# A graph network's first batch in another order: key chunks, adjacency rows, and who evicts

## The chip, the cores and the metric

The program runs on one core of a Trainium2 chip. The core has five engines that each work through their own list of instructions in order: TensorE (PE: matmuls and transposes; its weight loads are listed as PEld), VectorE (DVE), ScalarE (ACT), GpSimd (POOL) and SyncE (SP), which here only issues transfers. SBUF is the working memory, PSUM holds what TensorE writes. The metric is the device time of one execution in microseconds (us).

## The reference

Two layers over 16 graphs of 1024 nodes with 256 features. The adjacency matrix is symmetric, with ones on the diagonal. Every layer starts with `h = relu(layernorm(x))`.

```python
# layer 0
qkv = layer_norm(h, gamma1, beta1)            # 8 heads of 32
scores = qkv @ qkv.T / sqrt(32)               # by head
attn = softmax(where(adj > 0, scores, -inf))
h = h + attn @ qkv
y = layer_norm(h, gamma2, beta2)
x = x + h + gelu(y @ W1 + b1) @ W2 + b2
# layer 1
h = relu(layernorm(x))
t = h @ W
logits = (t @ a_1).T + t @ a_2 + (t @ a_12) @ t.T
att = softmax(where(adj > 0, leaky_relu(logits, 0.2), -9e15))
x = x + elu(h @ W_1 + (att @ h) @ W_2)
```

Queries, keys and values of layer 0 are one matrix, so its scores are symmetric.

## The kernel before

`fast_path` does the work; a second function is there for inputs that the first can't serve, and does not run. All 16 batches are written out one after another in one instruction stream, and the order that the program writes is kept on every engine.

**Units.** The attention of layer 0 goes in units. A unit is one half of the queries (512), one group of four heads and one tile of 128 keys: `scores` makes four blocks of 128 x 512 scores in two PSUM tiles, adds the mask, and takes exponentials; `weigh` multiplies the exponentials of the unit before with the values. Batch 0 has 32 units (2 query halves x 2 groups x 8 key tiles). In each of them TensorE adds the mask to the first two heads by a matmul with an identity, and VectorE adds it to the other two (line 1070); ScalarE takes the four exponentials (line 1077). Each of the two PSUM score tiles has one buffer. From batch 1 on the second half of the scores is taken from the symmetry ("mirrored"), VectorE adds all masks, and the units share TensorE with the matmuls of the MLP and of layer 1 of the batch before, which fill its time. Batch 0 has no batch before it.

**Preparing a batch** (`prologue`). The 1024 rows are four chunks of 256. For a chunk: `load`, `measure` "a" (statistics of x on VectorE, small steps on GpSimd), `rectify` (ScalarE: the normalized, clipped h), `measure` "b" (statistics of h), `value` (VectorE normalizes; GpSimd scales by gamma1 and adds beta1 into `va`), `turn` (TensorE transposes, ScalarE copies into `kT`). For chunks 0 and 1 of batch 0 `turn_normed` transposes before the scaling, ScalarE scales on the way out of PSUM, and GpSimd makes `va` afterwards (lines 838 to 853). Units 0 to 15 of batch 0 use queries of chunks 0 and 1; key tiles 4 to 7 (chunks 2 and 3) come from unit 4 on.

**Masks.** `fetch_mask` loads a tile of 128 adjacency rows as two halves of 256 KB; there are two such buffers. `convert_mask` (line 594, VectorE) makes 8-bit masks in `mq`, which has one buffer for a half of the queries (four tiles). A transposing transfer on SyncE turns each tile into `mk`. `turn_masks` does this for four tiles in six pieces: fetch 0; conversion 0 and fetch 1; transpose 0, conversion 1 and fetch 2; and so on. The first half of batch 0 has its own way, in `prologue`: four tiles of whole rows, 512 KB each, are loaded (`fetch`, line 884) and converted (`convert`, line 887). `compare_masks` then has GpSimd subtract mask and transposed mask (line 964); `collect` reduces the difference, by a square on ScalarE for the first half of the queries and by a maximum on VectorE for the second.

**Setup.** `setup` loads the weights and forms products of W, a_1, a_2 and a_12, with small evictions from PSUM on ScalarE (lines 678, 694).

**The order.** Each kind of work is a stream that yields places, and the piece with the lowest place is written next. Batch b's attention has places b to b + 1; in batch 0 one unit is 1/32 = 0.03125. `stream_c` places the preparation (that of batch 1 in 32 pieces from 0.34 to 0.85), `stream_m` the masks, `stream_s` the setup (0.25, 0.30, 0.35). `spread` lays n pieces between two places. Beside that, `defer` holds short follow-ups (a collection after a comparison: 3.0) until a planner's clock has gone on by so much; a unit of batch 0 counts 2.45. SyncE's transfers wait in SyncE's list for the buffers they need.

Of the kernel before, what the change touches and what calls it, by code (L numbers as in the profile page):

```python
# [495 lines left out]
def fast_path(  # L496
# [168 lines left out]
    def setup():  # L665
# [8 lines left out]
        for oc in range(DC):  # L674
            pt = ps_tile([P, DC, P], f"p_wT_{oc}")
            for ic in range(DC):
                nc.tensor.transpose(pt[:, ic, :], wl[:, ic, oc * P : (oc + 1) * P], ident)
            nc.scalar.copy(wT[:, oc, :], pt.rearrange("p c q -> p (c q)"))
        clock[0] += 0.5
        yield  # L680

        def product(dst, lhs, rhs, n, name):

            for oc in range(DC):
                pp = ps_tile([P, n], f"p_{name}_{oc}")
                for kc in range(DC):
                    matmul(
                        pp,
                        lhs[:, kc, oc * P : (oc + 1) * P],
                        rhs[:, kc, :n],  # L690
                        start=(kc == 0),
                        stop=(kc == DC - 1),
                    )
                nc.scalar.copy(dst[:, oc, :], pp)

        product(wb, wa, wT, D, "wb")
        clock[0] += 1.7
# [95 lines left out]
    def prologue(b, st):  # L793
# [30 lines left out]
        def value(i):  # L824
            mv, rs = stats["b", i]
            for j in range(TPC):
                t = i * TPC + j
                nrm = tmpp.tile([P, D], F32, tag="w1", bufs=6, name=f"nrm_{b}_{t}")
                normalize(nrm, h[t // TPH][:, t % TPH, :], mv, rs, j)
                if b == 0 and i < 2:  # L830
                    normed[t] = nrm
                    continue
                nc.gpsimd.tensor_mul(nrm, nrm, g1)  # L833
                nc.gpsimd.tensor_add(va[:, t, :], nrm, be1)
# [3 lines left out]
        def turn_normed(i):  # L838
# [7 lines left out]
            for g in range(NG):  # L846
                nc.scalar.activation(
                    kT[:, g, i * CW : (i + 1) * CW], pt[:, g, :], AF.Identity, bias=be1c[:, g : g + 1], scale=g1c[:, g : g + 1]
                )
            for j in range(TPC):  # L850
                t = i * TPC + j
                nc.gpsimd.tensor_mul(va[:, t, :], normed[t], g1)
                nc.gpsimd.tensor_add(va[:, t, :], va[:, t, :], be1)

        def turn(i):
            clock[0] += 0.5
            pt = ps_tile([P, NG, CW], f"ptk_{b}_{i}")
            for g in range(NG):
                for j in range(TPC):
                    nc.tensor.transpose(  # L860
                        pt[:, g, j * P : (j + 1) * P], va[:, i * TPC + j, g * P : (g + 1) * P], ident
                    )
            nc.scalar.copy(kT[:, :, i * CW : (i + 1) * CW], pt)

        steps = [
            load,
# [8 lines left out]
        if b == 0:  # L875
# [15 lines left out]

            load(0)
            load(1)
            for t in range(TPH):
                fetch(t)
                if t == 0:
                    for tile, src in first_rows:
                        nc.sync.dma_start(tile, src)
            load(2)
            load(3)  # L900
            measure(0, "a")
            measure(1, "a")
            rectify(0)
            rectify(1)
            measure(0, "b")
            measure(1, "b")
            value(0)
            turn_normed(0)
            convert(0)
            value(1)  # L910
            turn_normed(1)
            convert(1)
            convert(2)
            convert(3)
            yield
            for f in (lambda i: measure(i, "a"), rectify):
                for i in (2, 3):
                    f(i)
            yield
            measure(2, "b")  # L920
            value(2)
            yield
            measure(3, "b")
            value(3)
            yield
            for i in (2, 3):
                turns.append((1, lambda i=i: turn(i)))
                yield
            return
        for k in range(NCH + len(steps) - 1):  # L930
            for n in reversed(range(len(steps))):
# [24 lines left out]
    def compare_masks(b, qh, st):  # L956

        for half in range(qh + 1):
            for i in range(TPH):
# [10 lines left out]
                n = (b * 3 + qh + half) * TPH + i  # L970

                def collect(odd=odd, n=n):
                    if qh == 0:
                        nc.scalar.activation(odd, odd, AF.Square, accum_out=uneven[:, n : n + 1])
                    else:
                        nc.vector.tensor_reduce(
# [687 lines left out]
    def stream_c():  # L1664
        for b in range(B):
            if b == 0:
                yield -0.6
                for place, _ in zip((0.005, 0.032, 0.034, 0.07, 0.10, 0.13), prologue(b, states[b])):
                    yield place
            else:  # L1670
                yield from spread(prologue(b, states[b]), 32, b - 0.660, b - 0.150)

    def stream_m():
        for b in range(B):
            if b:
                start, end = (b - 0.28, b - 0.10) if b == 1 else (b - 0.73, b - 0.60)
                yield from spread(turn_masks(b, 0, states[b]), 5, start, end)
                yield from spread(compare_masks(b, 0, states[b]), TPH, end + 0.05, end + 0.14)
                yield from spread(turn_masks(b, 1, states[b]), 5, b + 0.02, b + 0.16)
                yield from spread(compare_masks(b, 1, states[b]), 2 * TPH, b + 0.17, b + 0.26)  # L1680
            else:
                yield from spread(compare_masks(b, 0, states[b]), TPH, b + 0.02, b + 0.2)
                yield from spread(turn_masks(b, 1, states[b]), 5, b + 0.23, b + 0.43)
                yield from spread(compare_masks(b, 1, states[b]), 2 * TPH, b + 0.52, b + 0.7)

    def stream_s():
        yield -0.3
# [82 lines left out]
```

## Time and profile before

| | us |
|---|---|
| median of 3 runs | 3312.72 (3311.82 to 3315.0) |
| profiled execution | 3314.71 |
| its span in the trace | 3312.9 |
| TensorE busy | 3227.3 |
| VectorE busy | 2580.9 |
| ScalarE busy | 2126.8 |
| GpSimd busy | 1667.5 |

A line of the trace names the engine, the line of the program, and what is written from what (`e<-s,mk`: the tile e from scores and mask). A count stands behind an x. In an answer on waits "A <- B" says that A's engine sat idle until B was done. In a timeline the first number is the start, the second the length. The granted clock is that of TensorE, 1.00 at full speed.

### The profile page before, as it was taken

What the parts mean: (1) busy time and instruction counts of PE and PEld (TensorE: products, weight loads), DVE (VectorE), ACT (ScalarE), POOL (GpSimd) and SP (SyncE); (2) the same over time, 40 slices, a digit from 0 to 9 for tenths busy, and PEclk for the clock granted to TensorE, in tenths of its full rate; (3) what the DMA queues carried; (4) which work ended last, traced back from release to release, by engine and by line L of the source; (5) the groups of instructions that cost most, each with busy time, mean ns of one, the idle gap of its engine ahead of it and who ended that gap; (6) DMA issues with size and microseconds to landing.
All of it is one profiled execution on the core that took longest, in us unless ns stands there. A gap on an engine that the chain in (4) does not pass through costs nothing. (4 is left out here: it accounts for less than half of the span.)

```text
span 3312.9 us, 115155 instructions
## 1 busy us (share of the span) xinstructions
PE 3227.3 (97%) x48866; PEld 1610.0 (49%) x48866; DVE 2580.9 (78%) x4565; ACT 2126.8 (64%) x5130; POOL 1667.5 (50%) x2397
## 2 busy tenths in 40 slices
PE   7799999999999999999999999999999999999998
PEld 2254445444454544445444454444445445454477
DVE  5687887888788788787878878888887887877734
ACT  7775765757667576675757667576675766657552
POOL 3564563736547265462745637365472655626120
PEclk9999999999999999999999999999999999999999
DMA  5264554645556464564645646455564645654400
GB/s 139 61 137 119 135 131 128 145 120 132 123 135 135 118 143 115 138 127 134 135 122 131 132 125 148 120 131 123 135 134 118 145 116 136 128 134 91 126 30 14
DMA packets 741706, 404.84 MB, mean 122 GB/s; under 512 B 173760, under 2 KB 700480, under 8 KB 741184
## 3 DMA queue, kind: packets, MB, share of 16 engines
q1 hardware_dynamic: 741184, 397.40, 50.5%
q8 instruction: 386, 6.32, 0.8%
q14 instruction: 136, 1.11, 0.1%
HBM read 233.97 MB, written 146.54 MB: 115 GB/s over the span
## 5 line engine op out<-in xcount | busy, mean ns | idle before, releaser
L1077 ACT ACTIVATE e<-e 128x512 f32<-128x512 f32 x1504 | 928.2, 618 | 502.5 <-DVE e L1070 498.0
L1070 DVE TENSOR_TENSOR e<-s,mk 128x1024 f32<-128x1024 f32 x748 | 879.6, 1216 | 124.4 <-PE s L1051 111.9
L574 PE MATMUL ph<-yT,w 128*32 128x256 f32 x7808 | 455.6, 381 | 11.1 <-DVE yT L1339 11.1
L574 PE MATMUL lg<-fT,uT 128*32 128x256 f32 x7680 | 450.1, 379 | 0.0
L574 PE MATMUL pa<-gw,e 128*32 128x258 f32 x7584 | 446.1, 380 | 0.0
L1051 PE MATMUL s<-kT 32*64 32x512 f32 x6272 | 444.3, 618 | 1.1 <-DVE e L1070 1.1
L1172 PE MATMUL o<-e,va 128*32 128x512 f32 x3136 | 443.8, 608 | 0.0
L574 PE MATMUL po<-w,hid 128*32 128x256 f32 x7680 | 434.5, 379 | 2.1 <-ACT hid L1363 1.6
L574 PEld LDWEIGHTS ph<-yT,w 128*32 128x32 f32 x7808 | 261.9, 110 | 204.1 <-DVE yT L1339 30.3
L574 PEld LDWEIGHTS po<-w,hid 128*32 128x32 f32 x7680 | 250.8, 110 | 204.8 <-issue 45.3
L574 PEld LDWEIGHTS lg<-fT,uT 128*32 128x32 f32 x7680 | 248.6, 110 | 197.9 <-issue 27.2
L574 PEld LDWEIGHTS pa<-gw,e 128*32 128x32 f32 x7584 | 246.2, 110 | 185.4 <-issue 22.1
L1106 POOL TENSOR_TENSOR part<-part,x 128x512 f32<-128x512 f32 x240 | 312.2, 1301 | 18.8
L1093 DVE STREAM_TRANSPOSE x<-e 128x1024 f32<-128x1024 f32 x240 | 290.6, 1226 | 35.7 <-ACT e L1077 27.8
L1456 DVE SCALAR_TENSOR_TENSOR e<-lg,gw,mk 128x256 f32<-128x256 f32 x512 | 222.7, 476 | 78.3 <-PE lg L574 69.2
L1077 ACT ACTIVATION_READ_ACCUMULATOR e<-e 128x1 f32 x1504 | 281.4, 187 | 0.0
L1462 ACT ACTIVATE e<-e,shift 128x512 f32<-128x512 f32 x256 | 183.1, 716 | 132.1 <-DVE e L1461 122.5
L833 POOL TENSOR_TENSOR nrm<-nrm,g 128x256 f32<-128x256 f32 x124 | 97.0, 782 | 308.3 <-DVE nrm L750 307.7
L1106 POOL TENSOR_TENSOR part<-x 128x512 f32<-128x512 f32 x120 | 156.7, 1306 | 178.2 <-DVE x L1093 178.1
L1363 ACT ACTIVATE hid<-ph,b1c 128x256 f32<-128x256 f32 x512 | 203.1, 463 | 56.8 <-PE ph L574 40.2
L1172 PEld LDWEIGHTS o<-e,va 128*32 128x32 f32 x3136 | 68.7, 108 | 337.4 <-issue 228.0
L594 DVE TENSOR_SCALAR mq<-adj 128x512 fp8e5<-128x512 int32 x248 | 188.8, 786 | 51.9 <-DMA adj<-in_adj_dram 50.6
(156 smaller groups left out, 4499.4 us busy)
## 6 DMA issues: line engine op xcount, KB each, us to landing
blocks<-x SPq DMA_DIRECT2D x480, 256.0 KB, 4.6
em<-blocks SPq DMA_DIRECT2D x240, 512.0 KB, 4.3
adj<-in_adj_dram SPq DMA_DIRECT2D x248, 256.0 KB, 3.6
h<-in_x_dram SPq DMA_DIRECT2D x64, 256.0 KB, 4.5
xb<-in_x_dram SPq DMA_DIRECT2D x128, 128.0 KB, 3.7
out_dram<-z SPq DMA_DIRECT2D x128, 128.0 KB, 4.1
rows<-row SPq DMA_DIRECT2D x120, 32.0 KB, 2.6
gather<-rows SPq DMA_DIRECT2D x120, 32.0 KB, 3.8
```

The source lines that it names most:

```text
L574: nc.tensor.matmul(out[c : c + HD], lhsT[:, c : c + HD], rhs, start=start, stop=stop)
L594: nc.vector.tensor_scalar(m[:, i * QW : (i + 1) * QW], a, 0.0, NEG8, op0=ALU.is_le, op1=ALU.mult, saturate=False)
L833: nc.gpsimd.tensor_mul(nrm, nrm, g1)
L1051: nc.tensor.matmul(sc[j // 2][c : c + P // 2, j % 2, :], kT[r, g, kt * P + c : kt * P + c + P // 2], kT[r, g, qs], start=j >= by_pe, stop= ...
L1070: nc.vector.tensor_tensor(e, masked, mask.unsqueeze(1).to_broadcast([P, 2, QW]), op=ALU.add)
L1077: nc.scalar.activation(e[:, j], masked[:, j], AF.Exp, scale=SCALE, accum_out=sums[kt // TPH, g][:, n, kt % TPH, qh : qh + 1],)
L1093: nc.vector.transpose(x[:, :, 2 * i : 2 * i + 2, :].rearrange("p c h j -> p h c j"), es[i].rearrange("p h (c i) -> p h c i", i=HD),)
L1106: add = lambda out, p, q: nc.gpsimd.tensor_tensor(out, p, q, op=ALU.add)
L1172: nc.tensor.matmul(o[j * HD : (j + 1) * HD, :], va[:, kt, (g * GH + j) * HD : (g * GH + j + 1) * HD], es[j // 2][:, j % 2, :], start=first ...
L1363: nc.scalar.activation(hid[:, f0 + i, :], ph[:, i, :], AF.Identity, bias=b1c[:, f0 + i : f0 + i + 1])
L1456: nc.vector.scalar_tensor_tensor(e[:, j, :], lg[:, j, :], gw[:, kt, D : D + 1], st[c // 2][:, kt // 2, qs, kt % 2], op0=ALU.add, op1=ALU.add,)
L1462: ready = defer(2.5, lambda: nc.scalar.activation(e, e, AF.Exp, bias=shift))
```

## The change

For batch 0, chunks 2 and 3 get the treatment of chunks 0 and 1 (`turn_normed`), and their loads stand ahead of adjacency tiles 1 to 3. Their statistics and rectification are written before unit 0; `value` and `turn_normed` of chunk 2 come after unit 0, those of chunk 3 after unit 1. GpSimd's scaling becomes a step of its own, `scale_values`. The conversions of the first four adjacency tiles come later, between the statistics.

In `stream_m` other places are given: comparisons of the first half of batch 0 at 0.10 to 0.16 (before 0.02 to 0.2); its second half fetched at 0.17 to 0.29 (0.23 to 0.43) and compared at 0.31 to 0.42 (0.52 to 0.7); batch 1's first half fetched at 0.45 to 0.58 (0.72 to 0.90) and compared at 0.63 to 0.72 (0.95 to 1.04); its second half fetched at 0.78 to 0.95 (1.02 to 1.16).

VectorE takes over from ScalarE the setup's evictions, the copies of batch 1's `turn`, and the collections of the first query half in batches 0 and 1.

```diff
-            nc.scalar.copy(wT[:, oc, :], pt.rearrange("p c q -> p (c q)"))
+            nc.vector.tensor_copy(wT[:, oc, :], pt.rearrange("p c q -> p (c q)"))
...
-                nc.scalar.copy(dst[:, oc, :], pp)
+                nc.vector.tensor_copy(dst[:, oc, :], pp)
...
-                if b == 0 and i < 2:
+                if b == 0:
                     normed[t] = nrm
                     continue
...
+        def scale_values(i):
             for j in range(TPC):
                 t = i * TPC + j
                 nc.gpsimd.tensor_mul(va[:, t, :], normed[t], g1)
...
-            nc.scalar.copy(kT[:, :, i * CW : (i + 1) * CW], pt)
+            (nc.vector.tensor_copy if b == 1 else nc.scalar.copy)(kT[:, :, i * CW : (i + 1) * CW], pt)
...
             load(0)
             load(1)
-            for t in range(TPH):
-                fetch(t)
-                if t == 0:
-                    for tile, src in first_rows:
-                        nc.sync.dma_start(tile, src)
+            fetch(0)
+            for tile, src in first_rows:
+                nc.sync.dma_start(tile, src)
             load(2)
             load(3)
-            measure(0, "a")
-            measure(1, "a")
-            rectify(0)
-            rectify(1)
-            measure(0, "b")
-            measure(1, "b")
+            for t in range(1, TPH):
+                fetch(t)
+            for i in range(2):
+                measure(i, "a")
+            for i in range(2):
+                rectify(i)
+            for i in range(2):
+                measure(i, "b")
             value(0)
             turn_normed(0)
-            convert(0)
+            for i in range(2, NCH):
+                measure(i, "a")
             value(1)
             turn_normed(1)
+            for i in range(2, NCH):
+                rectify(i)
+            convert(0)
             convert(1)
+            measure(2, "b")
             convert(2)
+            measure(3, "b")
             convert(3)
+            scale_values(0)
+            scale_values(1)
             yield
-            for f in (lambda i: measure(i, "a"), rectify):
-                for i in (2, 3):
-                    f(i)
+            value(2)
+            turn_normed(2)
             yield
-            measure(2, "b")
-            value(2)
+            value(3)
+            turn_normed(3)
             yield
-            measure(3, "b")
-            value(3)
+            scale_values(2)
             yield
-            for i in (2, 3):
-                turns.append((1, lambda i=i: turn(i)))
-                yield
+            scale_values(3)
             return
...
-                    if qh == 0:
+                    if qh == 0 and b > 1:
                         nc.scalar.activation(odd, odd, AF.Square, accum_out=uneven[:, n : n + 1])
...
-                for place, _ in zip((0.005, 0.032, 0.034, 0.07, 0.10, 0.13), prologue(b, states[b])):
+                for place, _ in zip((0.005, 0.032, 0.034, 0.063, 0.13), prologue(b, states[b])):
...
-                start, end = (b - 0.28, b - 0.10) if b == 1 else (b - 0.73, b - 0.60)
+                start, end = (b - 0.55, b - 0.42) if b == 1 else (b - 0.73, b - 0.60)
                 yield from spread(turn_masks(b, 0, states[b]), 5, start, end)
                 yield from spread(compare_masks(b, 0, states[b]), TPH, end + 0.05, end + 0.14)
-                yield from spread(turn_masks(b, 1, states[b]), 5, b + 0.02, b + 0.16)
+                start, end = (b - 0.22, b - 0.05) if b == 1 else (b + 0.02, b + 0.16)
+                yield from spread(turn_masks(b, 1, states[b]), 5, start, end)
...
-                yield from spread(compare_masks(b, 0, states[b]), TPH, b + 0.02, b + 0.2)
-                yield from spread(turn_masks(b, 1, states[b]), 5, b + 0.23, b + 0.43)
-                yield from spread(compare_masks(b, 1, states[b]), 2 * TPH, b + 0.52, b + 0.7)
+                yield from spread(compare_masks(b, 0, states[b]), TPH, b + 0.10, b + 0.16)
+                yield from spread(turn_masks(b, 1, states[b]), 5, b + 0.17, b + 0.29)
+                yield from spread(compare_masks(b, 1, states[b]), 2 * TPH, b + 0.31, b + 0.42)
```

## The prediction

> **What bounds the kernel now.** I read the busy table, then TensorE's waits, then the table by stretch, then the timelines of the first 180 us.
>
> ```profile
> PE 3227.3 (97%) x48866; PEld 1610.0 (49%) x48866; DVE 2580.9 (78%) x4565; ACT 2126.8 (64%) x5130; POOL 1667.5 (50%) x2397
> ```
>
> TensorE is idle for 85.6 of 3312.9 us. By stretch (columns: length, then busy time of PE, PEld, DVE, ACT, POOL, then granted clock):
>
> ```profile
> 0.00:20.00 20.00, 6.99 (x48) 2.40 (x56) 13.37 (x32) 8.08 (x18) 12.68 (x33) 1.00 0.85 199
> ...
> 80.00:100.00 20.00, 14.33 (x156) 3.38 (x156) 14.88 (x29) 13.52 (x41) 14.57 (x21) 0.85 0.00 1
> 100.00:120.00 20.00, 16.36 (x176) 4.77 (x168) 14.38 (x28) 14.37 (x44) 11.72 (x17) 0.89 0.15 34
> ...
> 160.00:180.00 20.00, 14.20 (x204) 6.49 (x204) 14.25 (x25) 14.35 (x31) 7.82 (x11) 0.83 0.62 149
> 180.00:200.00 20.00, 20.00 (x340) 10.04 (x336) 14.03 (x18) 12.39 (x31) 18.79 (x24) 1.00 0.68 120
> ```
>
> The nine stretches to 180 us hold 138.2 us of PE work, so 41.8 us of idle time, half of all. From there TensorE hardly waits, so a us won or lost before 180 us is a us of the end. The waits of the first 180 us (in total, times, longest):
>
> ```profile
> PE s L574 <- ACT e L1077: 18.1, 18, 4.4
> DVE mq L594 <- DMA adj<-in_adj_dram: 13.9, 10, 3.4
> ACT h L817 <- POOL nm L759: 13.3, 4, 5.2
> PE ph L574 <- DVE yT L1339: 6.0, 1, 6.0
> ```
>
> An undisturbed unit of batch 0 (units 4 to 5, 12 to 14) takes 3.08 us: mask and scores, ScalarE's first two exponentials, then the next unit's mask into the freed bank. I count by the starts of the mask matmuls: unit 0 at 14.18, 4 at 35.06, 8 at 48.00, 11 at 58.35, 15 at 73.45, 20 at 89.39, 24 at 110.69, 31 at 137.84. One stretch shows what a conversion that waits for its fetch does (VectorE's timeline; in brackets the idle time before):
>
> ```profile
> 127.18 0.43 DVE L594 TENSOR_SCALAR mq<-adj 128x512 fp8e5<-128x512 int32 x1 [0.33 <-DMA adj<-in_adj_dram]
> 129.40 0.43 DVE L594 TENSOR_SCALAR mq<-adj 128x512 fp8e5<-128x512 int32 x1 [1.79 <-DMA adj<-in_adj_dram]
> ...
> 130.92 1.22 DVE L1070 TENSOR_TENSOR e<-s,mk 128x1024 f32<-128x1024 f32 x1
> ```
>
> Unit 28's add stands behind it on VectorE; it came at 130.92 instead of 127.9, its exponentials waited, and units 28 to 30 took 8.70 us instead of 6.16.
>
> **The change, part by part** (minus is saved)
>
> *Start, units 0 to 4.* The two chunk loads now stand ahead of adjacency rows 1 to 3 on SyncE's queue. The transfer in that place was issued at 4.09 and took 8.7 us, so the chunks land by about 12.8. VectorE then: two measurements of 1.07 (18.51 to 19.58) end at 13.9, value(1) 0.75 at 14.65. Transposes, the key eviction of 1.02 and now four rectifications (2.08) put unit 0's exponentials at 18.5 (before 17.21). VectorE goes on in order: conversions 0 and 1 (0.68 each, in the cover of ScalarE), measurement 2b after the rectification at 17.5, conversion 2, measurement 3b, conversion 3: 20.55. Only then unit 0's adds of 1.29: 21.85 (before 18.59). Behind them stands value(2), 0.73, and TensorE's transposes of chunk 2 wait for it ahead of unit 1: 23.2 (before 18.52). With slow matmuls as in unit 1 before (1.04 + 2.01) unit 2 starts at 28.75 (before 25.70), but nothing is left to rectify, so units 3 and 4 follow at 3.08: 34.8 against 35.06. Gain 0.3. GpSimd's eight scalings of chunks 0 and 1 (0.73 to 0.83) move behind the statistics, about 21 to 27; unit 0's value product at 26 needs only the first, at 22.5. ScalarE's evictions of chunks 2 and 3 (1.02 each) lie beside TensorE's slow scores. SyncE's four transposes wait for conversions up to 20.6, so the weight loads queued behind start some 4 us later; they are needed only from 47 us. Bounds: -2 (chunks landing by 10.5) to +3 (conversions of 1.21 as three were before, and unit 2 still slow).
>
> *Collections of rows 0 to 3.* Four squares of 0.61 + 0.19 leave ScalarE in units 5 to 8, which took 9.86 instead of 9.24: -0.6. VectorE gets four reductions of 0.68; its idle 1.85 us a unit hides them.
>
> *First re-fetch, 0.17 to 0.29.* Six pieces lie 0.024 apart, a unit 0.03125. Pieces 1 and 2 (0.194 and 0.218) both fall between unit 6 (0.1875) and unit 7 (0.21875): conversion 0, its refetch and conversion 1 stand ahead of unit 7's add, conversion 2 ahead of unit 8's, conversion 3 ahead of unit 9's. Two buffers hold one row tile, so the fetch is issued when the conversion frees it. Measured: second tile done 5.3 us after the first (52.34 to 57.68), later ones 4.1 apart (125.29 to 129.40). After unit 6's add two collections also stand there (1.27). With add 6 ending at X: conversions end at X+2.0, 7.3, 11.4 and 15.5, and add 9 starts there (and after the setup's two evictions) instead of X+8.0. Some 0.5 us of this is slack, and the setup matmuls ahead of unit 10 (1.9 us) run partly in the wait. I get 64.3 to 65.0 for unit 11, against 58.35, 0.6 of it ahead already; with half clock after the wait (below): +7. Behind each late add stand the two exponentials of that unit on ScalarE, and TensorE's value product and next-but-one mask wait for these. Before, conversions lay 0.04 apart and cost 0.6 us. Bounds +4.5 (landing in the shortest 3.1 us instead of about 3.6) to +9.
>
> *Second, 0.45 to 0.58* (before 0.72 to 0.90). Pieces 2 and 3 fall between units 16 and 17, with a measurement (1.07) behind them. Counting from unit 15's mask: conversions end at 4.5, 9.9 and 13.9; add 17 starts at 15.0 instead of 8.0; conversion 3 ends at 18.0 and unit 20 starts at 21.2 against 15.9 before; half clock 1: +6.2. Bounds +3.5 to +8.5.
>
> *Half clock.* After the waits of 4.36 us (92.1 to 96.5) and 2.55 us (104.2 to 106.8) the granted clock was 0.50, and unit 21 took 4.53 us: 1.45 for a wait. [...]
>
> *GpSimd in units 20 to 24.* Four comparisons (1.15 each) of the eight that lay among the preparation of batch 1 go to units 9 to 13; four others take their place later. The rectification at 94.20 waited behind two comparisons, 3.17 us; without them about 1.3. Old stretch 21.3 us, new about 18.0: -3.3. Bounds -6.8 (both waits and half clocks gone) to 0.
>
> *Third, 0.78 to 0.95* (before 1.02 to 1.16). One piece a unit, as the second had: units 26 to 30 lose about 3.2, where units 24 to 30 lost 3.7 before. Four key copies go from ScalarE (0.57) to VectorE (about 0.68 as L1181's from PSUM); VectorE is the late engine there: +0.5 in all, bounds -1 to +2. The setup's eight small evictions lie in units 8 to 12 beside the conversion waits or TensorE's products; uncovered they cost about 3.
>
> *Batch 1's start.* The 6.0 us wait at 159.5 is yT behind conversions at 159.5 to 164.97. Gone, yT is done at 157.8 and TensorE runs to 162.4. Next late is ScalarE: activation-table load, gelu and load back (159.0 to 163.5, 0.8 earlier without the square ahead) stand ahead of unit 2's exponentials, so its product starts at 163.9 and the next block at 165.3 instead of 171.0: -5.7, bounds -7.7 to -3.
>
> Sum: -0.3 - 0.6 + 7 + 6.2 - 3.3 + 0.5 - 5.7 = **+3.8 us** on the profiled execution's 3314.71 (span 3312.9, 1.8 around it). That run lies 2.0 above the median of 3312.72, so the median becomes 3316.5; I say 3317.
>
> [...]
>
> **Rivals**
>
> *The fetches keep pace (faster).* If a tile came every 3.1 us the adds would not be late, both re-fetches would cost about 1, and the sum is -7.4: 3305. For it: the stretch at 36 to 52 us moves almost no bytes. Against it: the conversion at 57.25 waited there too, with only its own tile and a mask transpose under way. Chance 0.17.
>
> *The chunks land late (slower).* Before, chunk 3 landed at about 16.7, behind all adjacency rows. If small rows hold up the queue and it still does, value(1) and all of the start move 3.9 us; with half clock at unit 2 the sum is +9: 3322. It decides from a landing 1.4 us late (14.2) on, with that clock. Against it: its place in the queue. Chance 0.18.
>
> *Every re-fetched tile takes as long as the first (slower).* At 5.3 us a tile, with the mask transposes between the halves, conversion 3 ends 2.4 us later in the first stretch and conversions 2 and 3 some 2.4 in the second: +8.6, 3321. It decides from 4.7 us a tile. Against it: the 4.1 measured. Chance 0.15.
>
> *The saving at batch 1 is taken by ScalarE.* If gelu still ends at 163.5 and a wait halves the clock, 3 is left of 5.7: +6.5, 3319. Part of the middle case.
>
> **How the numbers follow.** Middle case 0.50 (own range 3310 to 3319), faster 0.17, the two slower rivals 0.33. All lower ends together make -10, all upper ends +19. The range reaches to both outer cases and leaves out about 1 in 10 on each side: from 3306, where half of the faster rival's chance lies below, to 3327, five above the slower ones. With 0.2% (6.6 us, about what a measurement of this kernel tells from no change): faster 0.17, within 0.50, slower 0.33.
>
> **What would show it.** Right: unit 4 near 35, no rectification between the exponentials of units 0 and 1; VectorE waiting on adjacency ahead of the adds of units 7 to 9 and 17, TensorE idle 3 to 5 us there; no wait for yT near 160. Wrong: conversions with no wait, unit 11 below 61, or unit 4 later than 38.

## The result and the profile after

The changed kernel takes 3321.05 us (median of 15 runs, 3314.37 to 3325.52); the kernel before takes 3313.51 beside it (15 runs, 3307.13 to 3316.59). The ratio is 1.0023, with an interval of 1.0016 to 1.0030: slower by 0.23%, some 7.5 us. The forecast was 3317, by a sum of +3.8 us. The other kernels below were run at other times, and the kernel before beside them has medians of 3309.75 to 3315.67 (these two on one and the same chip), so they are compared by their ratio to it.

The profiled execution has a span of 3319.6 us against 3312.9, 6.7 more. The busy table is almost the same. TensorE is busy for 3.0 us more with the same 48866 matmuls, and idle for 3.7 us more:

```profile
PE 3230.3 (97%) x48866; PEld 1610.2 (49%) x48866; DVE 2591.6 (78%) x4587; ACT 2120.3 (64%) x5102; POOL 1666.3 (50%) x2397
```

By stretch (length, busy time of PE, PEld, DVE, ACT and POOL, granted clock, DMA share, GB/s), the new loss lies at 40 to 60 us (TensorE busy for 17.93 before, 14.97 now), and the hole at 160 to 180 us closed (14.20 before, 18.56 now). At 80 to 100 us TensorE is as idle as before (14.33, now 14.03), but GpSimd, the late engine there before, is nearly idle (14.57, now 3.98). First the row of the kernel before at 40 to 60, then the changed kernel:

```profile
40.00:60.00 20.00, 17.93 (x231) 5.05 (x226) 9.38 (x11) 17.40 (x58) 0.00 (x0) 1.00 0.28 56
```

```profile
40.00:60.00 20.00, 14.97 (x148) 3.37 (x140) 11.73 (x17) 11.24 (x36) 3.55 (x4) 0.84 0.37 83
...
80.00:100.00 20.00, 14.03 (x147) 3.46 (x143) 12.93 (x27) 13.38 (x42) 3.98 (x11) 0.95 0.45 113
...
160.00:180.00 20.00, 18.56 (x243) 7.96 (x237) 12.06 (x17) 14.32 (x32) 10.68 (x15) 1.00 0.31 68
```

The waits of the first 180 us (in total, times, longest) tell the same by cause. Of ScalarE's waits, that for VectorE's adds has grown most, to 25.2 us from 16.3. TensorE's second half of scores now waits for these adds (7.4, before 1.1). `ACT h` behind GpSimd fell from 13.3 to 9.5, and the 6.0 us wait for yT is gone from the list. First two lines of the kernel before, then the changed kernel:

```profile
ACT e L1077 <- DVE e L1070: 16.3, 11, 3.5
...
PE s L1051 <- DVE e L1070: 1.1, 1, 1.1
```

```profile
ACT e L1083 <- DVE e L1076: 25.2, 14, 5.5
...
DVE mq L594 <- DMA adj<-in_adj_dram: 14.9, 15, 3.5
PE s L574 <- ACT e L1083: 12.7, 17, 2.9
...
ACT h L817 <- POOL nm L759: 9.5, 5, 5.2
...
PE s L1057 <- DVE e L1076: 7.4, 3, 3.8
```

(The lines of the program have moved by 6: the scores are L1057, the adds L1076, the exponentials L1083.)

The clearest stretch is the first re-fetch. On VectorE's timeline of the changed kernel (start, length, what, in brackets the idle time before), conversion 0 at 48.26 frees the buffer, the next tile's first half comes after a wait of 3.52 us, and the add of unit 7 (whose mask was at 47.16) stands behind both, until 54.46. Conversion 2 ends at 58.50 and conversion 3 at 62.82, each ahead of the add of one more unit:

```profile
45.93 1.23 DVE L1076 TENSOR_TENSOR e<-s,mk 128x1024 f32<-128x1024 f32 x1 [0.65 <-ACT e L1083]
47.07 1.27 DVE L982 TENSOR_REDUCE uneven<-odd 128x1 f32<-128x512 bf16 x2
48.26 0.75 DVE L594 TENSOR_SCALAR mq<-adj 128x512 fp8e5<-128x512 int32 x2
52.53 0.43 DVE L594 TENSOR_SCALAR mq<-adj 128x512 fp8e5<-128x512 int32 x1 [3.52 <-DMA adj<-in_adj_dram]
53.23 1.30 DVE L594 TENSOR_SCALAR mq<-adj 128x512 fp8e5<-128x512 int32 x1 [0.27 <-DMA adj<-in_adj_dram]
54.46 1.21 DVE L1076 TENSOR_TENSOR e<-s,mk 128x1024 f32<-128x1024 f32 x1
...
58.07 0.43 DVE L594 TENSOR_SCALAR mq<-adj 128x512 fp8e5<-128x512 int32 x1 [1.65 <-DMA adj<-in_adj_dram]
...
61.95 0.87 DVE L594 TENSOR_SCALAR mq<-adj 128x512 fp8e5<-128x512 int32 x1 [0.72 <-DMA adj<-in_adj_dram]
```

TensorE's side of it: the other half of unit 8's scores waits 3.76 us for that add, which frees their PSUM tile, and the matmuls behind the wait take twice as long (granted clock 0.50 from 55 to 60 us). Unit 9's mask comes at 59.34, 9 us after unit 8's:

```profile
50.33 0.61 PE L574 MATMUL s<-mk,ident 128*32 128x512 fp8e5 x8
50.87 1.09 PE L1057 MATMUL s<-kT 32*64 32x512 f32 x8
55.72 1.98 PE L1057 MATMUL s<-kT 32*64 32x512 f32 x8 [3.76 <-DVE e L1076]
57.63 1.94 PE L1178 MATMUL o<-e,va 128*32 128x512 f32 x8
59.34 1.08 PE L574 MATMUL s<-mk,ident 128*32 128x512 fp8e5 x8
```

Counted by the starts of the mask matmuls, as in the prediction:

| stretch | before | after | moved | forecast |
|---|---|---|---|---|
| start of unit 4 | 35.06 | 37.93 | +2.87 | -0.3 |
| units 4 to 8 | 12.94 | 12.40 | -0.54 | -0.6 |
| 8 to 11 (first re-fetch) | 10.35 | 17.05 | +6.70 | +7 |
| 11 to 15 | 15.10 | 15.60 | +0.50 | 0 |
| 15 to 20 (second) | 15.94 | 21.60 | +5.66 | +6.2 |
| 20 to 24 (GpSimd) | 21.30 | 17.73 | -3.57 | -3.3 |
| 24 to batch 1's first block (third) | 33.12 | 33.05 | -0.07 | +0.5 |
| batch 1, first to fifth block | 35.34 | 31.83 | -3.51 | -5.7 |
| from there to the end | | | -1.34 | 0 |
| sum | | | +6.70 | +3.8 |

### The profile page after: what moved, and what is told of

It is laid out like the page before. It is cut to its first block, busy times and chain, and to the rows that moved or that the text cites. A ratio compares the mean times of both kernels' runs of the same rounds, so it can differ in the third digit from the quotient of the medians.

```text
span 3319.6 us, 115147 instructions
## 1 busy us (share of the span) xinstructions
PE 3230.3 (97%) x48866; PEld 1610.2 (49%) x48866; DVE 2591.6 (78%) x4587; ACT 2120.3 (64%) x5102; POOL 1666.3 (50%) x2397
## 3 DMA queue, kind: packets, MB, share of 16 engines
q14 instruction: 135, 1.11, 0.1%
## 5 line engine op out<-in xcount | busy, mean ns | idle before, releaser
L1083 ACT ACTIVATE e<-e 128x512 f32<-128x512 f32 x1504 | 928.2, 618 | 506.5 <-DVE e L1076 502.0
L1076 DVE TENSOR_TENSOR e<-s,mk 128x1024 f32<-128x1024 f32 x748 | 879.4, 1215 | 110.6 <-PE s L1057 108.6
L1057 PE MATMUL s<-kT 32*64 32x512 f32 x6272 | 446.1, 618 | 7.4 <-DVE e L1076 7.4
L1083 ACT ACTIVATION_READ_ACCUMULATOR e<-e 128x1 f32 x1504 | 281.4, 187 | 0.0
L1369 ACT ACTIVATE hid<-ph,b1c 128x256 f32<-128x256 f32 x512 | 203.7, 463 | 62.8 <-PE ph L574 45.7
L970 POOL TENSOR_TENSOR odd<-mk,mq 128x512 bf16<-128x512 fp8e5 x192 | 219.4, 1161 | 23.0 <-PE s L1057 11.1
```

The costliest lines, as they stand in the source:

```text
L970: nc.gpsimd.tensor_tensor(odd.rearrange("p (u v x) -> p u v x", u=2, v=2), key.rearrange("p (u v x) -> p u v x", u=2, v=2), query.rearrang ...
L1057: nc.tensor.matmul(sc[j // 2][c : c + P // 2, j % 2, :], kT[r, g, kt * P + c : kt * P + c + P // 2], kT[r, g, qs], start=j >= by_pe, stop= ...
L1076: nc.vector.tensor_tensor(e, masked, mask.unsqueeze(1).to_broadcast([P, 2, QW]), op=ALU.add)
L1083: nc.scalar.activation(e[:, j], masked[:, j], AF.Exp, scale=SCALE, accum_out=sums[kt // TPH, g][:, n, kt % TPH, qh : qh + 1],)
L1369: nc.scalar.activation(hid[:, f0 + i, :], ph[:, i, :], AF.Identity, bias=b1c[:, f0 + i : f0 + i + 1])
```

## The experiments

The theory: the two early re-fetches cost some 12 us because VectorE, which works in order, waits for a tile whose fetch waits for a buffer that VectorE itself frees, with the adds of the units behind it. What the change gains (GpSimd's collisions, yT) is about 7 us, and the start costs what it costs because of the slow matmuls there. Each experiment is given as its edit, the expectation on record, and the measurement. In the table, "unit 4" and "block 5" are start times in the profiled execution (block 5: batch 1's fifth block of scores).

| kernel | ratio to before (95%) | unit 4 | 8 to 11 | 15 to 20 | 20 to 24 | 24 to 31 | block 5 |
|---|---|---|---|---|---|---|---|
| before | 1 | 35.06 | 10.35 | 15.94 | 21.30 | 27.15 | 179.15 |
| after | 1.0023 (1.0016 to 1.0030) | 37.93 | 17.05 | 21.60 | 17.73 | 24.88 | 187.19 |
| start_only | 1.0003 (0.9994 to 1.0012) | 35.89 | 10.35 | 15.95 | 21.81 | 25.47 | 178.00 |
| places_only | 1.0012 (1.0003 to 1.0021) | 34.87 | 13.53 | 21.55 | 17.77 | 24.44 | 179.88 |
| engines_only | 1.0005 (0.9996 to 1.0014) | 34.83 | 10.35 | 16.24 | 20.22 | 25.91 | 178.40 |
| fetch_ahead | 0.9989 (0.9980 to 0.9998) | 36.47 | 11.29 | 16.35 | 16.57 | 24.81 | 173.21 |
| value_late | 1.0009 (1.0000 to 1.0018) | 37.42 | 17.37 | 21.71 | 17.32 | 25.18 | 188.04 |
| start_warm | 0.9998 (0.9989 to 1.0007) | 34.30 | 17.52 | 22.00 | 16.24 | 26.27 | 183.33 |
| scalar_again | 1.0016 (1.0007 to 1.0025) | 38.08 | 13.60 | 22.39 | 17.80 | 26.13 | 184.95 |
| ahead_and_late | 0.9974 (0.9963 to 0.9986) | 36.86 | 11.29 | 16.34 | 17.36 | 24.64 | 172.36 |
| pieces_spaced | 1.0016 (1.0007 to 1.0025) | 38.07 | 12.49 | 17.49 | 17.45 | 27.13 | 181.16 |
| ahead_and_warm | 0.9973 (0.9963 to 0.9983) | 36.63 | 11.29 | 16.35 | 16.54 | 24.79 | 169.81 |

The ratio and block 5 of the one profiled execution agree only roughly. Set against the changed kernel they differ by up to 5.5 us: value_late is 4.6 us faster by its ratio and 0.85 later at block 5, and pieces_spaced is 2.3 faster by its ratio and 6.03 earlier at block 5. So differences of a few us between two kernels stand on the lengths of stretches, and on the time only where both agree.

### start_only: the start alone

The kernel before with the edits of `prologue` and of its places, and nothing else:

```diff
-                if b == 0 and i < 2:
+                if b == 0:
...
+        def scale_values(i):
...
-            for t in range(TPH):
-                fetch(t)
...
+            fetch(0)
...
+            value(2)
+            turn_normed(2)
```

> Only the new order of batch 0's preparation, with the places of masks and the engines of before. Theory 1 (the change is a sum of terms that stand side by side: start +2.9, re-fetches +6.7 and +5.7, GpSimd's collisions -3.6, batch 1's start -3.5 and -1.4, collections -0.5): unit 4 starts near 38 as in the changed kernel, unit 1 near 23.8 behind value(2), and the median is 2 to 5 us over before. Theory 2 (the start is paid back later by the slack of ScalarE in units 5 to 15): unit 4 late, but unit 15 within 1 us of before (73.45) and the median within 1 us.

Measured: 1.0003. Unit 1 starts 5.2 us later than before, as in the changed kernel (23.72), but unit 4 at 35.89 and not near 38, so the loss that the first theory expected is not there. The second theory's numbers came (unit 15 at 73.77, the median 0.57 us over). TensorE's timeline shows the difference. Here unit 1 runs at half speed and unit 2 is fast again (mask 0.61, scores 1.11):

```profile
22.09 0.47 PE L843 MATMUL ptk<-ident,nrm 128*128 128x128 f32 x1 [4.45 <-DVE nrm L750]
...
23.72 1.04 PE L574 MATMUL s<-mq,ident 128*32 128x512 fp8e5 x8
24.70 2.01 PE L1057 MATMUL s<-kT 32*64 32x512 f32 x16
...
29.74 0.61 PE L574 MATMUL s<-mq,ident 128*32 128x512 fp8e5 x8
30.29 1.11 PE L1057 MATMUL s<-kT 32*64 32x512 f32 x16
```

In the changed kernel, after the same wait of 4.45 us, unit 2 is slow as well:

```profile
22.16 0.48 PE L843 MATMUL ptk<-ident,nrm 128*128 128x128 f32 x1 [4.45 <-DVE nrm L750]
...
23.80 1.04 PE L574 MATMUL s<-mq,ident 128*32 128x512 fp8e5 x8
24.77 1.90 PE L1057 MATMUL s<-kT 32*64 32x512 f32 x16
...
30.46 1.04 PE L574 MATMUL s<-mq,ident 128*32 128x512 fp8e5 x8
31.43 1.98 PE L1057 MATMUL s<-kT 32*64 32x512 f32 x16
```

Its granted clock was 1.00 from 22 to 28 us and 0.50 from 30 to 32; in start_only it was 0.50 from 22 to 28 and 1.00 from 30. The work is the same and the wait of 4.45 us is the same; when the half clock comes differs. (The changed kernel has a second wait, of 1.31 us, ahead of unit 2, and start_only has none there. What part it has is not shown.) Five profiled executions have this start unaltered: unit 4 stands at 37.93 and 38.08 where unit 2 was slow (mask 1.04, in the changed kernel and in scalar_again), at 35.89 and 36.47 where it was not (0.61, in start_only and in fetch_ahead). In pieces_spaced it stands at 38.07.

### places_only: the places of the masks alone

```diff
-                start, end = (b - 0.28, b - 0.10) if b == 1 else (b - 0.73, b - 0.60)
+                start, end = (b - 0.55, b - 0.42) if b == 1 else (b - 0.73, b - 0.60)
...
-                yield from spread(compare_masks(b, 0, states[b]), TPH, b + 0.02, b + 0.2)
-                yield from spread(turn_masks(b, 1, states[b]), 5, b + 0.23, b + 0.43)
-                yield from spread(compare_masks(b, 1, states[b]), 2 * TPH, b + 0.52, b + 0.7)
+                yield from spread(compare_masks(b, 0, states[b]), TPH, b + 0.10, b + 0.16)
+                yield from spread(turn_masks(b, 1, states[b]), 5, b + 0.17, b + 0.29)
+                yield from spread(compare_masks(b, 1, states[b]), 2 * TPH, b + 0.31, b + 0.42)
```

> Only the new places of fetches and comparisons. Theory 1: unit 4 near 35.1; units 8 to 11 take 17 us instead of 10.35, units 15 to 20 about 21.6 instead of 15.94, units 20 to 24 about 17.7 instead of 21.3; no wait for yT near unit 2 of batch 1; the median 3 to 6 us over before. Theory 2 (the loss is the start's, the places are even): the median within 1.5 us of before.

Measured: 1.0012, the largest of the three parts, though their intervals overlap. The second re-fetch costs 5.61 us here (15.94 to 21.55) and GpSimd's stretch gains 3.53, both as in the whole change. The first one costs only 3.18 (13.53), but units 4 to 8 take 1.03 us longer than before, where the changed kernel saves 0.54. From unit 4 to unit 11 the places alone cost 4.21 us and the whole change 6.16. So about a third of it lies not in the places alone.

### engines_only: VectorE for ScalarE alone

```diff
-            nc.scalar.copy(wT[:, oc, :], pt.rearrange("p c q -> p (c q)"))
+            nc.vector.tensor_copy(wT[:, oc, :], pt.rearrange("p c q -> p (c q)"))
...
-                    if qh == 0:
+                    if qh == 0 and b > 1:
```

and the evictions of the setup's products and the key copies of batch 1 likewise.

> Only the evictions and collections moved to VectorE. Theory 1: units 5 to 8 take 9.3 instead of 9.86 us, all else as before; the median 0 to 1 us under before. Rival (VectorE is the late engine in units 24 to 30, so the copies there cost): the median 1 to 3 us over before.

Measured: 1.0005, no difference that can be told, so the time decides for neither theory. Unit 8 is reached 0.76 us earlier and block 5 0.75 earlier; units 24 to 31, where the rival had a loss, take 25.91 us instead of 27.15. The three parts alone make +0.03, +0.12 and +0.05%, together +0.20% beside the whole change's 0.23%, each of them uncertain by 0.09.

### scalar_again: the whole change without that part

The changed kernel with the four edits of engines_only taken back.

```diff
-            nc.vector.tensor_copy(wT[:, oc, :], pt.rearrange("p c q -> p (c q)"))
+            nc.scalar.copy(wT[:, oc, :], pt.rearrange("p c q -> p (c q)"))
...
-                    if qh == 0 and b > 1:
+                    if qh == 0:
```

> The changed kernel with the evictions and collections back on ScalarE. The places alone cost 3.2 us in units 8 to 11, the whole change 6.7. Theory 1 (the two collections and the setup's evictions stand in VectorE's list among the waiting conversions and push the chain of fetches): units 8 to 11 take 13.5 to 14 us instead of 17.05, the median 2 to 4 us under the changed kernel. Rival (the difference is half clock, which falls where it falls): units 8 to 11 still near 16 to 17.

Measured: units 8 to 11 take 13.60 us, as with the places alone (13.53), against 17.05. But unit 8 is 1.30 later (with the squares back on ScalarE, a mask waits 1.15 us for it), so from unit 4 to unit 11 the difference is 2.29 us (27.15 against 29.44). VectorE's collections and evictions, which alone save 0.76 us up to unit 8, thus cost some 2.3 once conversions that wait stand on the same engine. Counted from the start of unit 6's add, 1.2 of it is that the two reductions (at 47.07 above) stand ahead of conversion 0, with which the chain of fetches begins. Another 0.9 is that the chain took longer: from the end of conversion 0 to that of conversion 3 it is 13.8 us in the changed kernel and 12.9 here, for a reason that is not shown. The rival, the half clock, is there (0.50 from 54 to 60 us in the changed kernel, where the scores behind the wait take 1.98 us; here they take 1.09), but these conversions wait for transfers and not for TensorE. The second re-fetch took 0.79 more; block 5 is 2.24 earlier, and the ratio, 1.0016, overlaps the changed kernel's. The mechanism is shown in its stretch; a gain in time is not.

### fetch_ahead: no conversion waits for its own buffer

The changed kernel, with all eight transfers of each of the first two re-fetches issued at once into two idle tiles; conversions, comparisons and their places stay.

```diff
+        at_once = {}
+        if (b, qh) in ((0, 1), (1, 0)):
+            wide = [midp.tile([P, 2, N], I32, tag=f"mid{i}", name=f"adj_{b}_{qh}_{i}") for i in range(2)]
+            for i, t in enumerate(ts):
+                a = wide[i // 2][:, i % 2]
+                at_once[t] = b, t, [a[:, c : c + QW] for c in range(0, N, QW)]
+                for c in range(0, N, QW):
+                    nc.sync.dma_start(a[:, c : c + QW], rows(adj, b, t, slice(c, c + QW)))
```

> The changed kernel, with the adjacency of the first two re-fetches brought into two wide tiles of 16 KB a partition that stand idle in batch 0, all four row tiles at the first piece; conversions stay where they are. Nothing is left for them to wait for. Theory 1 (VectorE's adds are late because conversions wait for fetches that wait for a buffer): units 8 to 11 take about 10.5 us (17.05 in the changed kernel), units 15 to 20 about 16 (21.60), no half clock there, the median 9 to 13 us under the changed kernel, 3308 to 3312. Rival (conversions and collections are too much work for VectorE in these units, whatever the fetch): both stretches shorten by less than 2 us each, the median within 4 us of the changed kernel.

Measured: 0.9989, faster than before. VectorE's timeline of the same stretch as above has no wait for a fetch; the add of unit 7 comes at 49.10, where it came at 54.46, and that of unit 8 at 51.58, where it came at 59.08:

```profile
46.80 2.38 DVE L594 TENSOR_SCALAR mq<-adj 128x512 fp8e5<-128x512 int32 x4
49.10 1.21 DVE L1088 TENSOR_TENSOR e<-s,mk 128x1024 f32<-128x1024 f32 x1
50.24 0.75 DVE L594 TENSOR_SCALAR mq<-adj 128x512 fp8e5<-128x512 int32 x2
...
51.58 1.23 DVE L1088 TENSOR_TENSOR e<-s,mk 128x1024 f32<-128x1024 f32 x1
```

In the waits of its first 180 us the line of VectorE on adjacency transfers falls from 14.9 to 2.8 us. Units 8 to 11 take 11.29 (17.05), units 15 to 20 16.35 (21.60): 11.0 us of the two terms' 12.4 are gone, with the half clock behind the waits (1.00 from 50 to 60 us and from 92 to 104; no mask over 0.62 us and no scores over 1.11 from 80 to 100), and block 5 comes 13.98 earlier. The cost is the wait on the fetch; the new places themselves cost 0.9 and 0.4.

### pieces_spaced: the same buffers, pieces further apart

```diff
-                start, end = (b - 0.55, b - 0.42) if b == 1 else (b - 0.73, b - 0.60)
+                start, end = (b - 0.54, b - 0.36) if b == 1 else (b - 0.73, b - 0.60)
...
-                yield from spread(turn_masks(b, 1, states[b]), 5, b + 0.17, b + 0.29)
-                yield from spread(compare_masks(b, 1, states[b]), 2 * TPH, b + 0.31, b + 0.42)
+                yield from spread(turn_masks(b, 1, states[b]), 5, b + 0.17, b + 0.35)
+                yield from spread(compare_masks(b, 1, states[b]), 2 * TPH, b + 0.355, b + 0.455)
```

> The changed kernel with the pieces of its first two re-fetches laid further apart and nothing else: the first at 0.17 to 0.35 of the batch instead of 0.17 to 0.29, its comparisons at 0.355 to 0.455, the second at 0.46 to 0.64 instead of 0.45 to 0.58. Pieces are then 0.036 apart, more than the 0.031 of a unit, so that no two conversions stand ahead of one unit's adds. Theory (the cost is the bunching: a tile comes every 4.1 us through two buffers, and a second conversion in one unit makes that unit's adds wait for a whole fetch): a conversion every 3.6 us is late by some 0.5 us each, units 8 to 11 take 11 to 13 us instead of 17.05, units 15 to 20 16.5 to 18.5 instead of 21.60, and the time is 6 to 10 us below the changed kernel's ratio (0.9993 to 1.0005 of the kernel before instead of 1.0023). Rival (the order of transfers on the queue and the buffers' number decide, wherever the pieces stand): any four tiles through two buffers cost the same 5 to 7 us; the stretches only move, unit 24 is reached no earlier than 122.31 less 2 us, and the ratio stays at 1.0018 or above.

Measured: the stretches go as the theory said (12.49 and 17.49 us, both inside its ranges), and unit 24 is reached 6.57 us earlier than in the changed kernel. The time, 1.0016, is not: the theory had 1.0005 at most, and the rival's 1.0018 is nearer. But the rival's reason fell, since the stretches did not only move. Part of the gain was given back on GpSimd. The timeline of all engines around unit 14: four comparisons, now due here, stand ahead of the small step `nm` of batch 1's preparation; ScalarE's rectification waits 2.81 us for that, its exponentials stand behind it, and TensorE waits 3.82:

```profile
73.38 4.50 POOL L970 TENSOR_TENSOR odd<-mk,mq 128x512 bf16<-128x512 fp8e5 x4
...
78.28 0.19 POOL L759 TENSOR_TENSOR nm<-nm,rs_a 128x2 f32<-128x2 f32 x1
...
78.51 1.09 ACT L817 ACTIVATE h<-h,nm,rs_a 128x256 f32<-128x256 f32 x2 [2.81 <-POOL nm L759]
...
80.79 0.61 PE L574 MATMUL s<-mk,ident 128*32 128x512 fp8e5 x8 [3.82 <-ACT e L1083]
```

Units 11 to 15 took 17.83 us instead of 15.60, and units 24 to 31 27.13 instead of 24.88. It is the collision of comparisons and preparation that the change took away from units 20 to 24, made anew in unit 14. Even so block 5 comes 6.03 us earlier than in the changed kernel; that the ratio shows only some 2.3 us of this stays open.

### value_late: chunks 2 and 3 normalized one unit later

```diff
-                for place, _ in zip((0.005, 0.032, 0.034, 0.063, 0.13), prologue(b, states[b])):
+                for place, _ in zip((0.032, 0.063, 0.064, 0.066, 0.13), prologue(b, states[b])):
```

> The changed kernel, with value and turn_normed of chunks 2 and 3 written one unit later each (after units 1 and 2; chunk 2's keys are needed from unit 4). Theory 1 (unit 1 stands behind value(2) on VectorE and its transposes on TensorE): unit 1 starts near 19.5 instead of 23.8, unit 4 near 34 to 35 instead of 37.9, the median 2 to 5 us under the changed kernel. Rival (the start is bound by the adds behind conversions 2 and 3 and by half clock, wherever value(2) stands): unit 4 within 1 us of 37.9.

Measured: unit 1 starts at 20.68 instead of 23.80, unit 2 1.77 earlier, unit 4 only 0.52 earlier (37.42), and block 5 0.85 later. TensorE's order was not what held the start: the half speed of units 0 to 2 was there again (masks of 1.04), and VectorE's adds still stood behind the late conversions. In the trace the rival held. The ratio, 1.0009, is some 4.6 us below the changed kernel's, as the first theory had it, but its interval just touches the other's and nothing in this execution shows the gain, so it stays open.

### start_warm: work for TensorE in the wait

The changed kernel with 13 transposes that nothing reads, ahead of chunk 2's:

```diff
+            spare = ps_tile([P, P], "spare")
+            for _ in range(13):
+                nc.tensor.transpose(spare, ident, ident)
```

> The changed kernel with 13 more transposes of the identity into a spare PSUM tile while TensorE waits for value(2) ahead of unit 1 (extra work, nobody reads it). Theory 1 (part of the late start is half clock after the 4.45 us wait): matmuls of units 1 and 2 take 0.61 and 1.11 us instead of 1.04 and 1.9 to 2.0, unit 4 starts near 35 to 36, the median 1 to 3 us under the changed kernel. Rival (the extra transposes end late and hold the real ones up, or the clock does not go by TensorE's own work): units 1 and 2 as slow or later.

Measured: 0.9998. The wait falls from 4.45 to 2.92 us, units 1 and 2 run at full speed, and unit 4 starts at 34.30, 3.63 earlier than in the changed kernel:

```profile
17.68 1.69 PE L929 MATMUL spare<-ident 128*128 128x128 f32 x13
22.28 0.30 PE L843 MATMUL ptk<-ident,nrm 128*128 128x128 f32 x1 [2.92 <-DVE nrm L750]
...
23.47 0.61 PE L574 MATMUL s<-mq,ident 128*32 128x512 fp8e5 x8
24.02 1.11 PE L1060 MATMUL s<-kT 32*64 32x512 f32 x16
...
28.14 0.61 PE L574 MATMUL s<-mq,ident 128*32 128x512 fp8e5 x8
```

With units 1 and 2 at full speed the start beats the one before (35.06), although unit 1 still begins at 23.47. In this execution the whole loss of the start thus goes with the half speed and not with the order of VectorE's list. That the spare work is what keeps the clock up is not shown by one execution, as the last experiment tells. The ratio fell by 0.0025, some 8 us where the theory had 1 to 3, of which unit 4 and block 5 (3.86 earlier) show less than half.

### ahead_and_late and ahead_and_warm: towards a better kernel

ahead_and_late is fetch_ahead with the third re-fetch ahead too (`((0, 1), (1, 0), (1, 1))`) and the places of value_late.

> The changed kernel with all three re-fetches into the wide idle tiles and value of chunks 2 and 3 one unit later. Theory 1: against fetch_ahead (3308.7) units 24 to 31 lose their fetch waits too (about 3 us) and unit 4 is 3 us earlier: 3301 to 3306, under both kernels. Rival (units 24 to 31 are bound by something else, and the start's gain is lost again by unit 15): 3307 to 3310.

Measured: 3307.28 us, 0.9974 (0.9963 to 0.9986): faster than both kernels. That is 5 us under fetch_ahead by the ratio, as the first theory had it, and in the rival's range by absolute time (the kernel before was at 3315.67 here, and at 3312.04 beside fetch_ahead). Neither place of the gain came as the theory said: unit 4 is no earlier (36.86, in fetch_ahead 36.47), and units 24 to 31 take 24.64 us, against 24.81 in fetch_ahead and 24.88 in the changed kernel. The third re-fetch going ahead shows one step later: from unit 31 to batch 1's first block it takes 6.04 us, where fetch_ahead takes 7.92 and the changed kernel 8.17.

ahead_and_warm has all three re-fetches ahead, the changed kernel's places, and the spare transposes.

> The changed kernel with all three re-fetches of batches 0 and 1 going ahead into two idle tiles, as in ahead_and_late, its value products in the changed kernel's places, and 13 spare transposes of the identity on TensorE ahead of chunk 2's, as in start_warm. Theory (the half clock of units 0 to 2 and the waiting conversions are the two costs of the change, and they are apart): unit 4 starts at 34 to 34.6 instead of 37.93 (and 36.86 in ahead_and_late), unit 20 at 90 to 91, batch 1's fourth block near 170, and the time is 0.9965 to 0.9975 of the kernel before, 1 to 2.5 us below ahead_and_late's. Rival (what the start gains is given back to a later wait that hangs on GpSimd or the weight loads, not on TensorE): unit 4 at 34.3, but batch 1's fourth block at 172 or later, and the ratio at 0.9974 or above.

Measured: 3300.84 us where the kernel before takes 3309.75, 0.9973 (0.9963 to 0.9983). That is in the theory's range, but not 1 to 2.5 us below ahead_and_late, as it also said. Unit 20 (92.27) and unit 4 (36.63) come later than the theory said, block 5 (169.81; the expectation counts blocks from 0) where it said. Block 5 comes 2.55 us before ahead_and_late's. Behind TensorE's wait for y the matmuls were not slow here: from the transposes of y to the next transposes (`ptos`) it takes 9.42 us, in the changed kernel, where they were slow, 11.06, so 1.64 more. The spare transposes did not do this time what they did in start_warm: they took 1.91 us instead of 1.69, and unit 1 behind them ran at half speed (granted clock 0.50 from 22 to 28 us):

```profile
17.94 1.91 PE L929 MATMUL spare<-ident 128*128 128x128 f32 x13
...
24.08 1.04 PE L574 MATMUL s<-mq,ident 128*32 128x512 fp8e5 x8
25.06 2.01 PE L1072 MATMUL s<-kT 32*64 32x512 f32 x16
...
30.48 0.61 PE L574 MATMUL s<-mq,ident 128*32 128x512 fp8e5 x8
```

start_warm has a lower ratio than the same kernel without the spare transposes (0.9998 against 1.0023). For ahead_and_warm no such kernel was run: fetch_ahead (0.9989) lacks the third re-fetch ahead, and ahead_and_late (0.9974) has other places. So whether spare work helps, and by the clock, stays open.

## Why the prediction was right, and where it was not

**What held.** The two re-fetches: +7 and +6.2 were forecast, +6.70 and +5.66 came, by the mechanism described. The tiles' conversions ended 5.5, 4.0 and 4.3 us apart in the first stretch (49.0, 54.5, 58.5 and 62.8), where 5.3, 4.1 and 4.1 had been taken, and they stood ahead of the adds of units 7, 8 and 9, as said. In the second stretch the add of unit 17 came 12.9 us behind unit 15's mask and not 15.0, since the measurement stands behind it, while conversion 3 ended at 17.5 (forecast 18.0) and unit 20 began at 21.6 (21.2). fetch_ahead shows the cause: with the fetches ahead, 11.0 of these 12.4 us go. By places_only and scalar_again about a third of the first stretch (2.0 to 2.3 us of the 6.16 from unit 4 to unit 11) needs the collections and evictions on VectorE; the prediction had the two collections in its list ahead of conversion 0, but not as a cost of their own. The collections by themselves (-0.6 forecast, -0.54 measured) and GpSimd's collisions (-3.3, -3.57; places_only alone -3.53) came as said. The third re-fetch and the copies, +0.5, made -0.07. Two things lie in this that the prediction did not see apart: units 24 to 31 were 2.27 faster, and the way from unit 31 to batch 1's first block was 2.20 longer, since the wait of the last conversion fell late, and y behind it (TensorE waited 1.95 us for y at 154.39). With the third re-fetch ahead (ahead_and_late) that way is 6.04 us, against 5.97 before.

**The sum is nearer than its terms.** It was +3.8 against +6.70 in the profiled execution. Its terms were off by 5.9 us to one side (the start and batch 1's start above all) and by 3.0 to the other, so it is in part luck that it came within 3 us.

**The start was mis-sized: -0.3 forecast, +2.87 measured.** Nearly half of the error is the prediction's "units 3 and 4 follow at 3.08": it allowed slow matmuls in unit 1, and those of unit 2 were slow too, so that units 2 to 4 took 7.47 us, where they take 6.15 in start_only and 6.16 in fetch_ahead with a fast unit 2. In these two the start costs +0.8 to +1.4. The bound of +3 had "unit 2 still slow" in it, so the range took it in, but the value taken did not. The rest came ahead of unit 2, which starts at 30.46 and not at 28.75. The chunks were there earlier than reckoned (VectorE measured them from 11.01 on without a wait, not at 12.8). But value(2) and value(3) took 1.40 and 1.62 us, not 0.73, with GpSimd's scalings beside them, and TensorE waits for value(3) ahead of unit 2 too (1.31 us), which the prediction had only for value(2). The profile before had a row that tells: two such steps took 1.53 us there at 11.76, beside GpSimd's scalings. The rival "the chunks land late" fell; its time, 3322, was met for another reason.

**Batch 1's start: -5.7 forecast, -3.51 measured.** The wait for yT went as described, and the value product then waits 1.44 us for ScalarE behind gelu and its table loads, as forecast (1.5). From batch 1's second block to its fifth the saving is 5.15 us. Of the 2.2 that are missing, 1.64 lie before it: the matmuls behind the 1.95 us wait for y were slow,

```profile
154.39 0.33 PE L1341 MATMUL pty<-ident,y 128*128 128x128 f32 x1 [1.95 <-ACT y L769]
...
155.36 1.32 PE L1057 MATMUL s<-kT 32*64 32x512 f32 x16
156.61 1.94 PE L1178 MATMUL o<-e,va 128*32 128x512 f32 x8
158.31 7.70 PE L574 MATMUL ph<-yT,w 128*32 128x256 f32 x128
```

and in ahead_and_warm, behind a wait for y of 1.9 us, they were not:

```profile
139.63 1.11 PE L1072 MATMUL s<-kT 32*64 32x512 f32 x16
140.68 1.07 PE L1193 MATMUL o<-e,va 128*32 128x512 f32 x8
141.56 7.09 PE L574 MATMUL ph<-yT,w 128*32 128x256 f32 x128
```

Behind the same wait of 1.95 us the first scores took 2.01 us in fetch_ahead and 1.11 in places_only. The rival "the saving is taken by ScalarE" had about the right size (3 left of 5.7) for another reason: its half clock was to follow the wait for ScalarE, and the one that came lies behind the wait for y, before it.

**The other rivals.** "The fetches keep pace" fell with the waits of 3.5 us: it asked for a tile every 3.1 us, and in the first stretch of the changed kernel 4.0 to 5.5 were measured. "Every tile takes as long as the first" fell too: only the first took 5.5.

**The clock.** The prediction took its half clock from two waits of the kernel before, 4.36 and 2.55 us, with a granted clock of 0.50 behind them (behind the second it was 1.00 from 106 to 107 us, and 0.50 from 108 to 109). The length of a wait alone did not decide in these runs: behind 4.45 us the granted clock was 0.50 at once in start_only and only some 8 us later in the changed kernel, and behind 1.95 us scores took 2.01 us in fetch_ahead and 1.11 in places_only. What does decide is not shown. A term of this kind is a chance between two values, and the prediction took one of them.

## What to carry to other kernels

When a fetch waits for a buffer that a busy in-order engine frees, and that engine then waits for the fetch, a tile comes only every 4 to 5.5 us here, and all that stands behind it in that engine's list waits too. Look for idle memory to fetch ahead into before moving such a piece to another place; here two idle tiles turned a loss of 0.23% into a gain of 0.11%, and moving the pieces apart made a new collision on GpSimd (1.0016). An edit that is harmless alone (here: short reductions on an engine with spare time, 1.0005) can cost beside another (some 2.3 us here), since the short work delays the conversion that frees the buffer for the next fetch.

## What the runs showed that was not expected

TensorE's half speed is a matter of 2 us here and there, and differs between kernels with the same instructions and the same wait: five profiled executions with one start put unit 4 at 35.89 and 36.47, or at 37.93 to 38.08. So the end of a single profiled execution can't tell changes of 2 to 4 us in such a stretch; look at the durations of the matmuls behind the wait as well. And matmuls can run at half speed while the granted clock reads 1.00: units 0 and 1 of the changed kernel (masks 1.04, scores 2.01 and 1.90, at 14 to 18 and 24 to 27 us). VectorE's normalizing steps took twice as long (1.40 and 1.62 us for two, 0.74 at 10.35) when they lay beside GpSimd's scalings.
